# Packing diagonal score tiles and diagonal maxima tiles two to a set of four banks

## The chip, the core and the metric

The kernel runs on one core of one Trainium2 chip. The metric is the time of one execution in device microseconds (us); smaller is better. The engines are named as in the profile: PE is TensorE (PEld its weight loads), DVE is VectorE, ACT is ScalarE, POOL is GpSimd, and SP issues the DMAs. PSUM, into which PE writes, has eight banks of 512 float32 per partition here, called b0 to b7 in the kernel.

## The reference

One transformer block on 2048 tokens of 1024 features, in float32: layer norm with a modulation by a condition vector, causal attention with 32 query heads and 8 key heads of 32 features, a gated residual, a second modulated norm, and a low-rank mixture with one chosen expert of eight.

```python
mod = (_silu(L0_c) @ L0_wmod).reshape(L0_c.shape[0], 6, 1, -1)
...
h = _layernorm(x) * (1 + ca) + sa
q, k, v = h @ Wq, h @ Wk, h @ Wv          # 32 heads of q, 8 of k and v, head size 32
q, k = _apply_rope(q), _apply_rope(k)
scores = einsum('bhqd,bhkd->bhqk', q, k_h) / sqrt(32)
scores = where(causal, finfo.min, scores)  # key later than query is masked
ctx = einsum('bhqk,bhkd->bhqd', softmax(scores), v_h)
x = x + ga * (ctx @ Wo)
h = _layernorm(x) * (1 + cb) + sb
x = x + gb * low_rank_of_the_best_expert(h)
```

## The kernel before

The attention is done in 32 steps, one for each pair of a block of 512 queries (`qb`, 0 to 3) and a group of four heads (`m`, 0 to 7); `steps` holds them in the order of `qb`. In each product of the attention the four heads lie on four strips of 32 partitions, so that four matmuls of 32 partitions run beside each other, one for each head `j`, and each writes a bank of its own.

A step has these pieces, each known to the planner by a letter:

- **M, a visit of the maxima** (`unit` in `maxima_units`, L1406). It takes four banks, one for each head, computes the scores of one tile of 128 queries (`t`, 0 to 3) against 512 keys (`kc`), queries on partitions, and lets DVE reduce each bank to its row maxima (L1432). On the diagonal (`kc == qb`) only (t+1)·128 keys are computed: 128, 256, 384 or 512 columns. Before the products, 16 small bf16 matmuls write the mask of the diagonal 128x128 block (L1419); then L1426 adds the products.
- **R** (`shift_rows`): the maxima, negated and split into three bf16 parts by POOL (`split_maxima`, L1441 to L1447), are turned into rows by PE and copied by ACT (L1457).
- **S, a visit of the scores** (`weights`, L1472). It takes four banks and computes the scores again the other way round, 128 keys on partitions against 512 queries. L1479 writes minus the maximum with one matmul of bf16 ones for each head; on the diagonal L1487 adds the mask with 16 bf16 matmuls; L1492 adds the products. ACT takes the exponential of each bank into a tile `et` of SBUF (L1498). On the diagonal tile number `kc` begins at column `offset(kc)`: 0, 128, 256 or 384, so it is 512, 384, 256 or 128 columns wide. `nk` is the number of key tiles of a step: 4, 8, 12 or 16.
- **P** (`weighted_sum` and `accumulate`): PE multiplies `et` with the values into one bank `po` (L1508); POOL, in the last step DVE, adds `et` into `acc` (L1524 for the first two tiles, L1526 after that), except the last two tiles of a step.
- **D** (`denominators`, L1534): PE sums `acc` and the last two `et` tiles over the keys; then ACT, DVE and POOL divide (L1539, L1543, L1547).
- **F** and **T**: everything else of the block, cut into parts of some 0.4 to 1.9 us of PE: projections with the rotary turn (L675, L966, L844, L845), the output product (L675), transposes (L742), the second half of the block.

M and S use the array by rows: 32 partitions in, 128 columns out. P, D, R and most of F use it by columns: 128 partitions in, 32 columns out (the line's shape in the profile reads 32\*128 or 128\*32). The transposes use the whole array (128\*128). All float32 products go through the array in two passes, so that each appears twice in the profile's counts.

Buffers: `et` has four buffers (`epool`, bufs=4). A buffer comes free when POOL has added it and PE has used it; those of the last two tiles of a step come free with D. The eight banks are dealt out by the planner: an M or S takes four, P, D, R and F take one.

The order of the pieces is set before anything is issued by `plan_order` (L97), a beam search over states of the engines with a price for each piece, for each change of array form (`start`, L139), for each read of a bank and for each free buffer. It is the same order on all engines: PE, ACT, DVE and POOL each issue their instructions in it. `maxima` (L185), `scores` (L211), `sums` (L235) and `shares` (L258) are its pictures of M, S, P and D; `choices` (L327) tells which piece may come next, for instance S only while fewer than two scored tiles wait for their P (L340). The lists `ahead` and `tiles` (L1556 to L1566) tell it which M and S there are. The change alters the set of pieces, hence the search finds another order throughout.

Of the kernel before, what the change touches and what calls it, by code (L numbers as in the profile page):

```python
# [10 lines left out]
F32 = mybir.dt.float32  # L11
BF16 = mybir.dt.bfloat16
AF = mybir.ActivationFunctionType
# [83 lines left out]
def plan_order(parts, trail, steps, ahead, starts, tiles, ends, rates, gates):  # L97
# [87 lines left out]
    def maxima(s):  # L185
        n, t, kc = ahead[s[MAXIMA]]
        qb = steps[n][0]
        nk = QB if kc < qb else (t + 1) * P
        masked = kc == qb
        ready, turned = take(s, 4), unit_needs[s[MAXIMA]][1]  # L190
        if turned:
            ready = max(ready, s[TURNED][turned - 1] + TO_PE)
        s[PE] = start(s, "Rb" if masked else "R", ready) + 0.00167 * nk + (0.15 if masked else 0.0)
        s[WORK] += 0.00167 * nk
        after = s[PE] + TO_ENGINE
        give(s, *[(use(s, DVE, 0.07 + 0.00104 * nk, after) + TO_PE, b) for b in s[GOT]])
        s[MAXIMA] += 1
        if s[MAXIMA] - 1 == final[n]:
            done = use(s, POOL, 1.3, use(s, DVE, 0.15, 0.0) + BETWEEN)
            s[MINUS] = s[MINUS] + (done + TO_PE,)  # L200
# [10 lines left out]
    def scores(s):  # L211
        n, kc = tiles[s[SCORED]]
        if kc == 0:
            s[NOW] = n
            flush(s)
        width = QB - max(0, kc * P - steps[n][0] * QB)
        s[PE] = start(s, "Rb", max(take(s, 4), s[MINUS][n])) + 0.00209 * width
        s[WORK] += 0.00209 * width
        if kc >= 4 * steps[n][0]:
            s[PE] += 0.13  # L220
        free, s[ETS] = s[ETS][0], s[ETS][1:]
        after = max(s[PE] + TO_ENGINE, free)
        read = []
        for b in s[GOT]:
            done = use(s, ACT, 0.07 + 0.00083 * width, after)
            read.append((done + TO_PE, b))
        give(s, *read)
        s[READY] = s[READY][1:] + (done,)
        s[CREDIT] += rates[s[SCORED]]
        s[SCORED] += 1  # L230
# [4 lines left out]
    def sums(s):  # L235
        i = s[SUMMED]
        n, kc = tiles[i]
        nk = 4 * (steps[n][0] + 1)
        width = QB - max(0, kc * P - steps[n][0] * QB)
        ready = et_ready(s, i)  # L240
        at = ready + TO_PE
        if kc == 0:
            at = max(at, take(s, 1))
            s[SUM_BANK] = s[GOT][0]
        s[PE] = start(s, "C", at) + 0.00167 * width
        s[WORK] += 0.00167 * width
        if kc == nk - 1:
            give(s, (use(s, ACT, 0.5, s[PE] + TO_ENGINE) + TO_PE, s[SUM_BANK]))
        adder, us = (DVE, 0.0043) if n == last_step else (POOL, 0.00875)
        if kc == 1:  # L250
            s[ACC] = use(s, adder, us * QB, max(ready + BETWEEN, s[ACC_FREE]))
            free_et(s, max(s[ACC], s[PE]), 2)
        elif 1 < kc < nk - 2:
            s[ACC] = use(s, adder, us * width, ready + BETWEEN)
            free_et(s, max(s[ACC], s[PE]), 1)
        s[SUMMED] += 1
# [70 lines left out]
    def choices(s):  # L327
# [10 lines left out]
        if s[SCORED] < len(tiles):  # L338
            n, kc = tiles[s[SCORED]]
            if n < s[ROWS] and s[SCORED] - s[SUMMED] < 2 and not (s[SHARED] < n and kc > 1):  # L340
                found.append((max(four, s[MINUS][n] - 0.8), "S", scores))
        if s[SUMMED] < s[SCORED]:
            n, kc = tiles[s[SUMMED]]
            if not (s[SHARED] < n and kc == 1) and s[FILL] >= sums_need[s[SUMMED] > 0]:
                found.append((et_ready(s, s[SUMMED]) + TO_PE, "P", sums))
# [22 lines left out]
    for n, kc in tiles:  # L368
        span = starts[n + 2] - starts[n + 1] if n < last_step else 0.0
        due.append(starts[n + 1] + span * (kc + LEAD) / (4 * (steps[n][0] + 1)))  # L370
# [93 lines left out]
def adaln_block_kernel(  # L464
# [937 lines left out]
    def maxima_units(n):  # L1402

        qb, m = steps[n]

        def unit(t, kc):  # L1406
            nk = QB if kc < qb else (t + 1) * P
            if n not in maxima:
                maxima[n] = two.tile([P, 4, 4, NQB], F32, tag="mx", name=f"mx_{n}")
            mx = maxima[n]  # L1410
            q, k = quad(m, qb), k_t[:, m // 4, :]
            masked = kc == qb
            ps = score_banks(f"sm_{n}_{t}_{kc}")

            if masked:
                for s in range(4):
                    o = t * P + s * HD
                    for j, rows in groups:
                        nc.tensor.matmul(  # L1419
                            ps[j][:, o : o + HD], later[rows, s, :],  # L1420
                            pick[rows, s, s * HD : (s + 1) * HD], start=(s == 0), stop=False,
                        )
            spans = [(t * P, nk), (0, t * P)] if masked and t else [(0, nk)]
            for a, b in spans:
                for j, rows in groups:
                    nc.tensor.matmul(  # L1426
                        ps[j][:, a:b], q[rows, t * P : (t + 1) * P],
                        k[rows, kc * QB + a : kc * QB + b], start=not masked,
                        stop=(a, b) == spans[-1],
                    )  # L1430
            for j in range(4):
                nc.vector.tensor_reduce(mx[:, t, j : j + 1, kc], ps[j][:, :nk], AX.X, ALU.max)  # L1432

        units = [lambda t=t, kc=kc: unit(t, kc) for t in range(4) for kc in range(qb + 1)]
        return units

# [22 lines left out]
    class Attend:  # L1459
        def __init__(self, n):  # L1460
            self.n = n
            self.qb, self.m = steps[n]
            self.nk = 4 * (self.qb + 1)
            self.ets = {}

            last = n == len(steps) - 1
            self.adder = nc.vector if last else nc.gpsimd
# [4 lines left out]
        def weights(self, kc):  # L1472

            off, qb = self.offset(kc), self.qb
            q, k, nt = quad(self.m, qb), k_t[:, self.m // 4, :], nts[self.n % 2]
            ps = score_banks(f"sc_{self.n}_{kc}")

            for j, rows in groups:
                nc.tensor.matmul(  # L1479
                    ps[j][:, off:], ones_h[rows, :], nt[rows, off:],  # L1480
                    start=True, stop=False,
                )
            if kc >= 4 * qb:
                for s in range(4):
                    w = (s + 1) * HD
                    for j, rows in groups:
                        nc.tensor.matmul(  # L1487
                            ps[j][:, off : off + w],
                            pick[rows, s, :], later[rows, s, :w], start=False, stop=False,
                        )  # L1490
            for j, rows in groups:
                nc.tensor.matmul(  # L1492
                    ps[j][:, off:], k[rows, kc * P : (kc + 1) * P], q[rows, off:],
                    start=False, stop=True,
                )
            et = epool.tile([P, 4, QB], F32, tag="et", name=f"et_{self.n}_{kc}")
            for j in range(4):
                nc.scalar.activation(  # L1498
                    et[:, j, off:], ps[j][:, off:], AF.Exp, scale=1.0 / math.sqrt(HD)
                )  # L1500
            self.ets[kc] = et

        def weighted_sum(self, kc):
            off, et = self.offset(kc), self.ets[kc]
            if kc == 0:
                self.po = bank(f"po_{self.n}")
            for j, rows in groups:
# [3 lines left out]
                    start=(kc == 0), stop=(kc == self.nk - 1),  # L1511
                )
            if kc == self.nk - 1:
                nc.scalar.copy(quad(self.m, self.qb), self.po)

        def accumulate(self, kc):

            off, et = self.offset(kc), self.ets[kc]
            if kc == 1:
# [5 lines left out]
            elif 1 < kc < self.nk - 2:  # L1525
                self.adder.tensor_add(self.acc[:, :, off:], self.acc[:, :, off:], et[:, :, off:])  # L1526

        def denominators(self):
            pd = bank(f"pd_{self.n}")
            parts = [(0, self.acc)]  # L1530
            parts += [(self.offset(kc), self.ets[kc]) for kc in (self.nk - 2, self.nk - 1)]
# [25 lines left out]
    for n, (qb, m) in enumerate(steps):  # L1557
        ahead += [(n, t, kc) for t in range(4) for kc in range(qb + 1)]
# [7 lines left out]
    tiles = [(n, kc) for n in range(len(steps)) for kc in range(4 * (steps[n][0] + 1))]  # L1566
    attend = [Attend(n) for n in range(len(steps))]
    ends = [sum(s.nk for s in attend[: n + 1]) for n in range(len(steps))]
# [23 lines left out]
    for n, t, kc in ahead:  # L1592
        qb, m = steps[n]
        b = 2 * qb + t // 2
# [13 lines left out]
        parts, [k for k, _ in trail], steps, ahead, starts, tiles, ends, rates, gates  # L1608
# [5 lines left out]
    for letter, banks in order:  # L1614
# [15 lines left out]
        elif letter == "S":  # L1630
            n, kc = tiles[i]
            now[0] = n
            attend[n].weights(kc)
        elif letter == "P":
            n, kc = tiles[i]
# [68 lines left out]
```

## Time and profile before

| | |
|---|---|
| median of 3 runs | 1782.79 us (1782.09 to 1783.23) |
| the profiled execution | 1782.16 us |
| its span, first to last instruction | 1780.4 us |
| around the span | 1.8 us |
| PE busy | 1747.0 us (98%) |
| POOL busy | 1185.1 us (67%) |
| DVE busy | 1094.3 us (61%) |
| ACT busy | 740.0 us (42%) |
| mean granted clock of PE | 0.996 |

The span is what the profile covers; the time of an execution has 1.8 us more. Busy time is counted from the first to the last moment of an instruction, and the ends of matmuls are modelled, so a PE that is busy for 98% of the span may still spend part of that on filling and emptying the array. What a visit costs PE is better read from the timeline: from the start of its first matmul to the start of the first matmul after it.

### The profile page before, as it was taken

The page shows a single profiled execution, that of the slowest core. Times are in us where ns is not written, and L with a number is a line of the kernel's source. Part 1 is how long each engine was busy: PE and PEld are TensorE (multiplying, and loading weights), DVE is VectorE, ACT ScalarE, POOL GpSimd, SP SyncE. Part 2 cuts the span into 40 slices and gives each one's busy share as a digit, 9 for nine tenths or more (in the row PEclk, how much of TensorE's full clock was granted, in tenths as well). Part 3 has the DMA queues.
Part 4 walks back from the last instruction along what each step waited for, and adds up shares of the span by engine and source line. Part 5 has one row for each costly group of instructions (what it writes and reads, how often), then busy time and mean ns, then how long its engine had stood idle before and what let it go on. Part 6 is the DMA issues. An engine that isn't in the chain of part 4 may idle for free.

```text
span 1780.4 us, 55951 instructions
## 1 busy us (share of the span) xinstructions
PE 1747.0 (98%) x25112; PEld 708.9 (40%) x25112; DVE 1094.3 (61%) x2160; ACT 740.0 (42%) x1634; POOL 1185.1 (67%) x568
## 2 busy tenths in 40 slices
PE   7999999999999999999999999999999999999997
PEld 3655555444444333334444343333333333333333
DVE  2455456755755674676475566575566765666497
ACT  1203334344433424455444333454544444455452
POOL 1233343487567649657885866978979778798852
PEclk9999999999999999999999999999999999999999
DMA  9512323212422421131103011101102111110101
GB/s 350 181 30 74 115 80 103 73 50 62 137 73 96 153 87 49 49 102 61 61 26 125 26 49 68 41 37 49 49 25 73 37 61 49 49 49 25 49 13 49
DMA packets 68496, 130.57 MB, mean 73 GB/s; under 512 B 3744, under 2 KB 20768, under 8 KB 68256
## 3 DMA queue, kind: packets, MB, share of 16 engines
q1 hardware_dynamic: 66928, 125.85, 20.5%
q8 instruction: 196, 3.21, 0.8%
q10 hardware_dynamic: 1328, 1.15, 0.2%
q14 instruction: 44, 0.36, 0.1%
HBM read 118.59 MB, written 8.39 MB: 71 GB/s over the span
## 4 chain that ended last, share of the span: by engine, by line
PE 88%; POOL 6%; DVE 2%; issue 2%; DMA 1%; ACT 1%; POOLq 0%; ACTq 0%; DVEq 0%
PE sm L1426 15%; PE po L1508 14%; PE sc L1492 12%; PE pw L675 11%; PE pq L966 11%; PE sc L1479 5%; POOL acc L1526 5%; PE pd L1534 3%; PE pk L675 3%; PE pv L675 2%; PE pa L675 2%; PE open L966 2%; PE pf L675 2%; PE sm L1419 1%; DVE mx L1432 1%
## 5 line engine op out<-in xcount | busy, mean ns | idle before, releaser
L1432 DVE TENSOR_REDUCE mx<-sm 128x1 f32<-128x512 f32 (+3 forms) x1280 | 689.0, 602 | 397.7 <-PE sm L1426 396.2
L1498 ACT ACTIVATE et<-sc 128x512 f32<-128x512 f32 (+3 forms) x1280 | 578.4, 540 | 705.5 <-PE sc L1492 701.3
L1526 POOL TENSOR_TENSOR acc<-acc,et 128x2048 f32<-128x2048 f32 (+1 forms) x180 | 792.8, 4404 | 31.8 <-ACT et L1498 22.8
L1426 PE MATMUL sm<-k_t,q 32*128 32x512 f32 (+3 forms) x3328 | 336.6, 475 | 3.0 <-ACT et L1498 3.0
L1492 PE MATMUL sc<-q,k_t 32*128 32x512 f32 (+3 forms) x2560 | 297.2, 536 | 0.0
L1508 PE MATMUL po<-et,v_sb 128*32 128x512 f32 (+3 forms) x2560 | 294.8, 538 | 0.1
L675 PE MATMUL pw<-w,q 128*32 128x512 f32 x1920 | 238.7, 598 | 0.0
L1524 POOL TENSOR_TENSOR acc<-et,et 128x2048 f32<-128x2048 f32 (+1 forms) x31 | 132.1, 4261 | 98.5 <-ACT et L1498 83.1
L966 PE MATMUL pq<-h_t,w 128*32 128x256 f32 x3072 | 191.9, 384 | 0.0
L1426 PEld LDWEIGHTS sm<-k_t,q 32*128 32x128 f32 x3328 | 139.5, 184 | 116.9 <-issue 43.5
L966 PEld LDWEIGHTS pq<-h_t,w 128*32 128x32 f32 x3072 | 90.5, 110 | 100.6 <-issue 44.8
L1508 PEld LDWEIGHTS po<-et,v_sb 128*32 128x32 f32 x2560 | 59.0, 108 | 175.5 <-issue 152.3
L1543 DVE RECIPROCAL rd<-rd 128x128 f32<-128x128 f32 x128 | 112.4, 919 | 18.9 <-ACT rd L1539 18.8
L1479 PE MATMUL sc<-nt,ones_h 32*128 32x512 bf16 (+3 forms) x1280 | 120.1, 352 | 3.5 <-ACT rd L1539 2.9
L1112 POOL TENSOR_TENSOR x<-ag,x 128x512 f32<-128x512 f32 x40 | 60.9, 1523 | 87.3 <-DVE ag L1111 87.3
L1492 PEld LDWEIGHTS sc<-q,k_t 32*128 32x128 f32 x2560 | 115.5, 185 | 5.8 <-issue 2.1
L1479 PEld LDWEIGHTS <-ones_h 32*128 32x128 bf16 x1280 | 32.9, 91 | 207.6 <-issue 201.5
L844 POOL TENSOR_TENSOR swap_q<-swap_q,cs 128x512 f32<-128x512 f32 x32 | 40.9, 1277 | 105.7 <-DVE swap_q L841 105.7
L675 PEld LDWEIGHTS pw<-w,q 128*32 128x32 f32 x1920 | 50.1, 109 | 129.3 <-issue 110.8
L1547 POOL TENSOR_TENSOR q<-q,rd 128x512 f32<-128x512 f32 x31 | 41.6, 1343 | 67.3 <-DVE rd L1543 49.5
L1111 DVE TENSOR_TENSOR ag<-pw,gate 128x512 f32<-128x512 f32 x40 | 27.5, 687 | 62.5 <-PE pw L675 60.9
L844 POOL TENSOR_TENSOR swap_k<-swap_k,cs 128x512 f32<-128x512 f32 x8 | 10.2, 1276 | 82.7 <-DVE swap_k L841 82.7
(146 smaller groups left out, 1340.0 us busy)
## 6 DMA issues: line engine op xcount, KB each, us to landing
w<-in_wo_dram SPq DMA_DIRECT2D x112, 256.0 KB
w<-in_wmod_dram SPq DMA_DIRECT2D x48, 512.0 KB
w<-in_wq_dram SPq DMA_DIRECT2D x48, 512.0 KB
x<-in_x_dram SPq DMA_DIRECT2D x32, 512.0 KB
out_dram<-x SPq DMA_DIRECT2D x16, 512.0 KB
w<-in_wv_dram SPq DMA_DIRECT2D x12, 512.0 KB
w<-in_wk_dram SPq DMA_DIRECT2D x12, 512.0 KB
wq<-in_wq_dram SPq DMA_DIRECT2D x8, 512.0 KB
```

The costliest lines, as they stand in the source:

```text
L675: nc.tensor.matmul(dst[rows], left[:, rows], right, start=start, stop=stop)
L966: nc.tensor.matmul(ps[j * HD : (j + 1) * HD, a * TB : (a + 1) * TB], self.query_weights(half, k, j * P + h * HD), self.h_t[:, k, :], start ...
L1112: nc.gpsimd.tensor_add(x1[t][:, cols], tmp, x1[t][:, cols])
L1426: nc.tensor.matmul(ps[j][:, a:b], q[rows, t * P : (t + 1) * P], k[rows, kc * QB + a : kc * QB + b], start=not masked, stop=(a, b) == spans ...
L1432: nc.vector.tensor_reduce(mx[:, t, j : j + 1, kc], ps[j][:, :nk], AX.X, ALU.max)
L1479: nc.tensor.matmul(ps[j][:, off:], ones_h[rows, :], nt[rows, off:], start=True, stop=False,)
L1492: nc.tensor.matmul(ps[j][:, off:], k[rows, kc * P : (kc + 1) * P], q[rows, off:], start=False, stop=True,)
L1498: nc.scalar.activation(et[:, j, off:], ps[j][:, off:], AF.Exp, scale=1.0 / math.sqrt(HD))
L1508: nc.tensor.matmul(self.po[rows, off:], v_sb[:, kc, 4 * (self.m // 4) + j, :], et[:, j, off:], start=(kc == 0), stop=(kc == self.nk - 1),)
L1524: self.adder.tensor_add(self.acc[:, :, off:], first[:, :, off:], et[:, :, off:])
L1526: self.adder.tensor_add(self.acc[:, :, off:], self.acc[:, :, off:], et[:, :, off:])
L1543: nc.vector.reciprocal(part, part)
```

## The change

On the diagonal, pieces that do not fill their four banks are put together so that two of them fill one set of banks.

- Maxima: in all steps but the first two, query tile 0 (128 columns) and query tile 2 (384 columns) share one visit; tiles 1 and 3 stay alone. `unit` takes a tuple of tiles `ts`; `unit_list` names the visits. DVE still makes one reduction for each tile and head.
- Scores: in every step the key tiles nk-3 (384 columns) and nk-1 (128 columns) share one visit; the tile nk-2 (256 columns) comes after them. The narrow tile's columns lie at 384 to 511, the wide one's are moved to 0 to 383. Both `et` tiles are taken in this visit. ACT still makes one exponential for each tile and head. The P of the three tiles follow the new order.
- Planner: a visit may hold several tiles; it waits for all the `et` buffers that it needs, and S is offered only when that many are free. The mask's price in a maxima visit goes from 0.15 for each visit to 0.18 for each tile.

```diff
@@ plan_order: choices
-            n, kc = tiles[s[SCORED]]
-            if n < s[ROWS] and s[SCORED] - s[SUMMED] < 2 and not (s[SHARED] < n and kc > 1):
+            n, kc, _ = tiles[s[SCORED]]
+            k = packs[s[SCORED]]
+            if (
+                n < s[ROWS] and s[SCORED] - s[SUMMED] < 2 and not (s[SHARED] < n and kc + k > 2)
+                and len(s[ETS]) >= k
+            ):
                 found.append((max(four, s[MINUS][n] - 0.8), "S", scores))
@@ maxima_units: unit
-        def unit(t, kc):
-            nk = QB if kc < qb else (t + 1) * P
+        def unit(ts, kc):
...
-            ps = score_banks(f"sm_{n}_{t}_{kc}")
+            ps = score_banks(f"sm_{n}_{ts[0]}_{kc}")
+            runs, at = [], 0
+            for t in ts:
+                runs.append((t, at, at + ((t + 1) * P if masked else QB)))
+                at = runs[-1][2]
             if masked:
-                for s in range(4):
-                    o = t * P + s * HD
+                for t, at, _ in runs:
+                    for s in range(4):
+                        o = at + t * P + s * HD
...
             for j in range(4):
-                nc.vector.tensor_reduce(mx[:, t, j : j + 1, kc], ps[j][:, :nk], AX.X, ALU.max)
+                for t, a, b in runs:
+                    nc.vector.tensor_reduce(mx[:, t, j : j + 1, kc], ps[j][:, a:b], AX.X, ALU.max)
@@ unit_list (new)
+        qb = steps[n][0]
+        if n < 2:
+            return [((t,), 0) for t in range(4)]
+        out = []
+        for t in range(4):
+            out += [((t,), kc) for kc in range(qb)]
+            out += [((), ((1,), qb), ((0, 2), qb), ((3,), qb))[t]] if t else []
+        return out
@@ Attend
+            self.order = [*range(self.nk - 2), self.nk - 1, self.nk - 2]
+            self.packs = [[kc] for kc in self.order]
+            self.packs[-3:-1] = [self.order[-3:-1]]
...
-        def weights(self, kc):
+        def weights(self, kcs):
...
+            runs = [(kc, self.offset(kc), self.offset(kc), QB) for kc in kcs]
+            if len(runs) > 1:
+                kc, off, _, _ = runs[0]
+                runs[0] = (kc, off, 0, QB - off)
...
+            for kc in kcs:
+                self.ets[kc] = epool.tile([P, 4, QB], F32, tag="et", name=f"et_{n}_{kc}")
             for j in range(4):
-                nc.scalar.activation(
-                    et[:, j, off:], ps[j][:, off:], AF.Exp, scale=1.0 / math.sqrt(HD)
-                )
+                for kc, off, a, b in runs:
+                    nc.scalar.activation(
+                        self.ets[kc][:, j, off:], ps[j][:, a:b], AF.Exp, scale=1.0 / math.sqrt(HD)
+                    )
```

Within a shared visit the matmuls of one kind stand together: in S the bf16 ones of both tiles, then the masks of both, then the products of both; in M the masks of both, then the products of both.

## The prediction

> **What bounds the kernel now.** I read the page first: whose time is it?
>
> ```profile
> span 1780.4 us, 55951 instructions
> PE 1747.0 (98%) x25112; PEld 708.9 (40%) x25112; DVE 1094.3 (61%) x2160; ACT 740.0 (42%) x1634; POOL 1185.1 (67%) x568
> ...
> PE 88%; POOL 6%; DVE 2%; issue 2%; DMA 1%; ACT 1%; POOLq 0%; ACTq 0%; DVEq 0%
> ```
>
> PE is busy for 98% of the span and makes 88% of the chain that ended last; no other engine is near. The granted clock is 0.996 on the mean, so it cannot rise. PE's own time is therefore the time, and the question is what of it is not products. The change removes no matmul: the two programs, whose instruction order can be read without running them, both hold 15,636. It removes visits, so I read the timeline for what a visit costs beyond its columns. Each duration below is from a group's first start to the next group's first start.
>
> ```profile
> 818.13 0.40 PE L1479 MATMUL sc<-nt,ones_h 32*128 32x512 bf16 x4
> ...
> 819.52 1.50 PE L675 MATMUL pv<-w,h_t 128*32 128x256 f32 x24
> 820.95 1.14 PE L1426 MATMUL sm<-k_t,q 32*128 32x512 f32 x8
> ...
> 823.02 0.34 PE L1479 MATMUL sc<-nt,ones_h 32*128 32x384 bf16 x4
> ...
> 824.15 1.07 PE L1508 MATMUL po<-et,v_sb 128*32 128x512 f32 x8
> ...
> 826.90 2.37 PE L675 MATMUL pk<-h_t,w 128*32 128x256 f32 x40
> 829.20 0.29 PE L1479 MATMUL sc<-nt,ones_h 32*128 32x256 bf16 x4
> ```
>
> Leaving the column form: 24 records took 819.52 to 820.95, 1.43 us; 40 took 826.90 to 829.20, 2.30 us. So 8 records are 0.435 us, three times that is 1.305, and some 0.13 us is left each time before a row visit starts (0.139 in the trace's nanoseconds).
>
> ```profile
> 1309.66 0.40 PE L1479 MATMUL sc<-nt,ones_h 32*128 32x512 bf16 x4
> ...
> 1310.84 1.07 PE L675 MATMUL pw<-w,q 128*32 128x512 f32 x8
> ...
> 1313.35 0.40 PE L1479 MATMUL sc<-nt,ones_h 32*128 32x512 bf16 x4
> ...
> 1314.44 1.03 PE L1426 MATMUL sm<-k_t,q 32*128 32x512 f32 x8
> 1315.39 1.07 PE L1534 MATMUL pd<-acc,ones_p 128*32 128x512 f32 x8
> ```
>
> Leaving the row form: the same scores visit takes 1.18 us ahead of a column product, 1.09 us ahead of another row visit (1.183 and 1.084 in nanoseconds): 0.099 us. A full maxima visit took 0.955 us behind a row visit here and 1.071 us in the usual row behind column work: 0.115 us more, because it opens with float32 products. A scores visit, which opens with bf16, pays 0.009.
>
> Do two tiles side by side then really save this, with masks on both? One place shows it, two masked scores visits that follow each other:
>
> ```profile
> 236.70 0.40 PE L1479 MATMUL sc<-nt,ones_h 32*128 32x512 bf16 x4
> ...
> 238.00 0.33 PE L1479 MATMUL sc<-nt,ones_h 32*128 32x384 bf16 x4
> ...
> 239.11 1.27 PE L966 MATMUL pq<-h_t,w 128*32 128x256 f32 x17
> ```
>
> Together 2.41 us; apart 1.39 (818.13 to 819.52) and 1.13 (823.02 to 824.15), 2.52. The difference 0.11 is one way out and in again of the row form; masks and products add up.
>
> **The change part by part.**
>
> *Visits.* 30 steps lose one maxima visit each, 32 steps one scores visit each: 640 become 578. If each had stood alone between column runs, that were 62 x (0.139 + 0.099 + 0.009) = 15.3 us. But the search orders everything anew, so I count in the two orders. Runs of row work: 588 before, 536 after (52 fewer). Runs of column work: 588 and 543 (45 fewer). Whole-array transposes: 63 and 63. Maxima without a mask at the head of a row run: 165 and 170; scores at the head: 305 and 275. Sum: 52 x 0.099 = 5.1; 45 x 0.139 = 6.3; minus 5 x 0.115 = 0.6; plus 30 x 0.009 = 0.3. **11.1 us less on PE**, all on the path.
>
> Here a rule of the Trainium skill stands behind the row. "TensorEngine Tiling (Array Packing)", Key Properties, says that changing the tiling mode drains the array; "TensorE: Matmul & The Clock Gate", the phases on the wall clock, puts the drain at some 128 cycles, 53 ns at 2.4 GHz. An estimate by that page alone: 97 changes x 0.053 = 5.1 us. The rows show 139 and 99 ns, more than a drain; the trace's durations count.
>
> *Masks, products, weight loads*: the same instructions, costed at nothing more by the 2.41 us above. No row shows two maxima masks side by side; a maxima visit of 128 columns takes 0.516 us (0.302 beyond its 0.214 of columns), one of 384 columns 0.950 (0.308 beyond). From none to the 0.2 us of a mask lost again over 30 visits is 0 to +6 us; I take 0, by the scores' row.
>
> *DVE and ACT*: the same number of reductions and exponentials.
>
> ```profile
> L1432 DVE TENSOR_REDUCE mx<-sm 128x1 f32<-128x512 f32 x896 | 554.9, 682 | 279.3 <-PE sm L1426 278.3
> L1432 DVE TENSOR_REDUCE mx<-sm 128x1 f32<-128x384 f32 x128 | 62.3, 549 | 44.9 <-PE sm L1426 44.7
> L1432 DVE TENSOR_REDUCE mx<-sm 128x1 f32<-128x128 f32 x128 | 28.1, 281 | 32.9 <-PE sm L1426 32.7
> ```
>
> A shared maxima visit holds its last bank for 4 x (281 + 549) = 3.3 us of DVE, a full one for 4 x 682 = 2.7. The exponentials: 282 and 504 ns against 603, so 3.1 against 2.4 us. A rule speaks against the change here: "PSUM — Partial Sum Buffer", PSUM bank collisions, wants a bank guarded as a bank, not by address, so the narrow tile's readers start only when the wide tile is done as well. If every shared visit paid its 0.65 us on PE, 62 x 0.65 = 40 us. But the next row visit must stand close behind to feel it. Pairs of row visits with nothing between fall from 52 to 42, those with under 0.7 us of work between from 37 to 18, under 1.0 us from 214 to 209; some 60 of 577 are close, so 40 x 60 / 577 = 4 us at most. On the other side, 29 close pairs fewer, at 0.1 us each (the usual maxima behind scores takes 1.05 us against 0.955), give 3 us back. I take 0, with +4 and -3 for the range.
>
> *The added wait.* A shared scores visit needs two `et` buffers at once: its first exponentials need those freed by the sums nk-7 and nk-6. ACT runs in order: behind a waiting exponential stand the copies of L1457, L1514, L1539 and the other exponentials, and four banks stay taken, for which PE's next row visit waits. POOL's addition takes 4.5 us. In the timeline of before, in the 24 steps with `qb` over 0, addition nk-6 ended after the first exponential of tile nk-3 in 7 steps, by 0.4 to 3.8 us, 12 us in all. The new order puts 16.5 us of PE work between S of nk-6 and the shared visit, 13.8 before; with 2.7 us more room only 1.1 and 0.4 of the lags are left, under 2 us. Hidden by column work, mostly: I take 0, with +5 for the range. Without the cover it would be all 12.
>
> *The end of a step.* Its last exponentials are 256 wide now, not 128: 4 x (389 - 282) = 0.4 us later, ahead of P and D. Other work stands there on PE (in the last step 14 parts of the output product follow); without it, 32 x 0.4 = 14 us. I take 0.
>
> *Moved work.* Projections, weight loads on SP's queue and rotary work on POOL move with the order; DMA has 1% of the chain. What can change is where chance waits fall. Summed over all visits, PE took 43 us more than the usual durations of the same visits; 14 of that lie in the opening and the ending, 29 between, among them 5.2 us at 959 (ACT stood behind the rotary table's sign, L832, which came late) and 3.3 at 178 (ACT's L1539 behind POOL's L1547). These are dealt anew: 0, give or take 5.
>
> *Sum.* 1782.16 of the profiled execution (span 1780.4 and 1.8 around it) - 11.1 = 1771.1; that execution lay 0.6 below the median, so **1771.7**, which I round to 1771.5.
>
> **The rivals.**
> - *More than the count*: the big chance waits do not come back (-8) and close pairs give 3: 1761 to 1767. For it: fewer close pairs. Against: new orders bring new waits.
> - *The wait for `et` eats most of it*: +5 to +9, 1776 to 1781. For it: 7 late additions, POOL busy at 80% and more behind 1060 us. Against: the 2.7 us of room.
> - *Slower, by the same wait without room*: if POOL's addition nk-6 is late at every shared visit of the 24 by 1 us net of cover, +24 - 11 = +13, 1795. It decides from 11.1 / 24 = 0.46 us of net wait for each. Against: in 17 of 24 steps the addition was done in time, and work on PE lies between.
> - *It does not do what it says*: a second set of masks, or the stretch between bf16 and float32, costs a change of form again; then 1781 to 1784. Against: 2.41 us at 236.70.
>
> **How the numbers follow.** Count as worked: 0.60, 1767 to 1776. More: 0.19. Wait eats most: 0.11, of which 0.01 ends within 0.2%. No saving: 0.05. Slower: 0.05. A difference of 0.2%, 3.6 us, is about what a measurement of this kernel tells from none. Faster 0.60 + 0.19 + 0.10 = 0.89, same 0.05 + 0.01 = 0.06, slower 0.05. The range of 8 in 10 takes the likeliest case with the bounds above (+4, +5, -3, and 5 either way, not all at once): 1764 to 1779.
>
> **What would show it.** In the timeline after, a shared scores visit of 384 and 128 columns ahead of a column product should take 1.13 + 0.59 - 0.11 = 1.61 us (0.594 is the usual one of 128 columns), a shared maxima visit 0.95 + 0.52 - 0.10 to 0.11 = 1.36. Row runs: 536. PE's busy time falls by some 5 to 11 us. The groups L1432 and L1498 keep counts and means. Wrong: shared visits dearer by 0.1 or more (masks), ACT's idle time with POOL's L1526 as releaser (the `et` wait), or PE's row visits over their usual durations by clearly more than 29 us between opening and ending.

## The result, and the profile after

The changed kernel takes 1765.06 us (median of 5 runs, 1762.35 to 1766.24) against 1782.79 us before: a ratio of 0.9901, 95% interval 0.9888 to 0.9915, or 17.7 us less. The forecast was 1771.5, with a range of 1764 to 1779. The profiled execution took 1763.81 us, its span 1762.0, so span against span the change brought 18.4 us.

The page after, its span, the busy row and the chain by engine:

```profile
span 1762.0 us, 56024 instructions
PE 1728.6 (98%) x25112; PEld 718.8 (41%) x25112; DVE 1089.4 (62%) x2160; ACT 737.9 (42%) x1634; POOL 1176.2 (67%) x568
...
PE 78%; POOL 15%; issue 3%; DVE 1%; DMA 1%; ACT 1%; SPq 0%; POOLq 0%; ACTq 0%; DVEq 0%
```

PE's busy time fell by 18.4 us, as much as the span, with the same 25,112 records. PE stays the bound: the chain runs over POOL's additions for more of its length (15% for 6%), but PE is as full as before, 98%. The mean granted clock of this execution is 0.999, against 0.996 before.

The timeline of PE after, columns as before (start, length, engine, line, operation, operands, count), around one shared scores visit:

```profile
1004.01 0.40 PE L1521 MATMUL sc<-nt,ones_h 32*128 32x384 bf16 x8
1004.24 0.47 PE L1529 MATMUL sc<-later,pick 32*128 32x32 bf16 x32
1004.54 1.09 PE L1535 MATMUL sc<-q,k_t 32*128 32x384 f32 x16
1005.56 1.06 PE L1553 MATMUL po<-et,v_sb 128*32 128x512 f32 x8
```

Twice the ones, twice the masks, twice the products, and one way back into the column form: 1004.01 to 1005.56, 1.55 us (1.554 is the median of the 26 that stand between column runs). The prediction had worked out 1.61. A shared maxima visit:

```profile
985.18 0.37 PE L1434 MATMUL sm<-pick,later 32*128 32x32 bf16 x32
985.39 1.19 PE L1447 MATMUL sm<-k_t,q 32*128 32x128 f32 x24
986.51 1.72 PE L686 MATMUL pk<-h_t,w 128*32 128x256 f32 x28
```

985.18 to 986.51, 1.33 us (1.331 is the median of the 19 that stand so), where 1.36 was worked out. So both are cheaper than the sum of their parts, by 0.057 and 0.026 us.

The readers on DVE, groups of the reductions by shape (busy us, mean ns, idle before):

```profile
L1454 DVE TENSOR_REDUCE mx<-sm 128x1 f32<-128x512 f32 x896 | 554.5, 682 | 282.4 <-PE sm L1447 281.7
L1454 DVE TENSOR_REDUCE mx<-sm 128x1 f32<-128x384 f32 x128 | 69.4, 546 | 2.8 <-PE sm L1447 2.8
L1454 DVE TENSOR_REDUCE mx<-sm 128x1 f32<-128x128 f32 x128 | 35.5, 282 | 63.2 <-PE sm L1447 63.0
```

The counts are those of before and the means nearly so (682, 549 and 281 ns). DVE now waits 63 us ahead of the narrow reductions and 2.8 ahead of the wide ones (32.9 and 44.9 before), as it would if it started on both when the shared visit is done. Together the idle time ahead of the two did not grow: 77.8 us before, 66.0 now. On ACT the exponentials of the shared visits take a little longer than before: 515 ns for 504 at 384 columns, 309 for 282 at 128.

To tell work from waiting I took every visit or run of PE work in the traces (from its first start to the next one's first start) and fitted one duration for each record of a kind and width, one for each change of form and one for each kind of opening, over all traces of this study together, leaving out those off by more than 20 ns. The sum of these is called *usual*; what the trace took beyond it is called *waits*, opening and ending included. It is a fit, good to about 1 us between kernels, and stands in no view of the profile. The rest of the span, some 15 us, lies ahead of the first matmul and behind the start of the last run. (The prediction had 43 us of waits for the kernel before, by another count; only figures of one and the same count can be compared.)

| kernel | span us | usual us | waits us | median us |
|---|---|---|---|---|
| before | 1780.4 | 1707.7 | 57.5 | 1782.8 |
| after | 1762.0 | 1693.4 | 53.6 | 1765.1 |
| difference | -18.4 | -14.3 | -3.9 | -17.7 |

14.3 us are work that PE no longer does, 3.9 us are fewer waits. What this count calls waits includes time in which PE works at a lower granted clock, and that is where the 3.9 us seem to lie. The profile of before has two such stretches between the opening and the ending (95 to 1730 us), from 184.25 to 187.66 us and from 962.49 to 969.31, both at a granted clock of 0.50; the profile after has none there. Each follows, or begins within, a wait of some 3 us:

```profile
182.88 0.32 PE L1479 MATMUL sc<-nt,ones_h 32*128 32x384 bf16 x1 [2.94 <-ACT rd L1539]
...
183.98 2.58 PE L966 MATMUL pq<-h_t,w 128*32 128x256 f32 x24
...
963.48 2.24 PE L1426 MATMUL sm<-k_t,q 32*128 32x512 f32 x4 [3.00 <-ACT et L1498]
```

The 24 records at 183.98 take 2.58 us, while 24 records of the same shape take 1.50 at 819.52 in the prediction's lines. PE had work in 9.2 of these 10.2 us, so the lower clock cost some 4.6 us (an estimate: half of 9.2). Without it the waits are 52.9 us before and 53.6 after. The executions on record say the same: 33 of the kernel before, taken with experiments 1 to 4, have a mean clock of 0.995, and the time rises by some 1.3 us for each 0.001 of clock lost; the five of the changed kernel have 0.998. So some 4 of the 17.7 us go with the clock (an estimate: 0.003 at that rate). At the same clock, 0.997, three executions of before took 1779.55 to 1780.09 us and one of the changed kernel 1765.06, some 14.7 less.

### The profile page after: what moved, and what is told of

It reads as the page before. It is cut to its first block, busy times and chain, and to the rows that moved or that the text cites. A ratio compares the mean times of both kernels' runs of the same rounds, so it can differ in the third digit from the quotient of the medians.

```text
span 1762.0 us, 56024 instructions
## 1 busy us (share of the span) xinstructions
PE 1728.6 (98%) x25112; PEld 718.8 (41%) x25112; DVE 1089.4 (62%) x2160; ACT 737.9 (42%) x1634; POOL 1176.2 (67%) x568
## 4 chain that ended last, share of the span: by engine, by line
PE 78%; POOL 15%; issue 3%; DVE 1%; DMA 1%; ACT 1%; SPq 0%; POOLq 0%; ACTq 0%; DVEq 0%
PE sm L1447 13%; POOL acc L1571 12%; PE pq L977 12%; PE po L1553 11%; PE sc L1535 10%; PE pw L686 8%; PE sc L1521 4%; PE pv L686 3%; PE pd L1579 3%; PE pk L686 3%; PE open L977 2%; PE pa L686 2%; PE mr L792 1%; PE pf L686 1%; PE sm L1434 1%
## 5 line engine op out<-in xcount | busy, mean ns | idle before, releaser
L1447 PE MATMUL sm<-k_t,q 32*128 32x512 f32 (+3 forms) x3328 | 327.7, 473 | 0.0
L1535 PE MATMUL sc<-q,k_t 32*128 32x512 f32 (+3 forms) x2560 | 290.4, 533 | 0.5 <-issue 0.5
L686 PE MATMUL pw<-w,q 128*32 128x512 f32 x1920 | 234.7, 598 | 4.0 <-DMA w<-in_wo_dram 4.0
L977 PE MATMUL pq<-h_t,w 128*32 128x256 f32 x3072 | 186.8, 382 | 0.0
L1447 PEld LDWEIGHTS sm<-k_t,q 32*128 32x128 f32 x3328 | 135.6, 184 | 124.6 <-issue 50.9
L1123 POOL TENSOR_TENSOR x<-ag,x 128x512 f32<-128x512 f32 x40 | 53.0, 1325 | 134.2 <-DVE ag L1122 134.0
L1553 PEld LDWEIGHTS po<-et,v_sb 128*32 128x32 f32 x2560 | 63.9, 109 | 164.8 <-issue 140.3
L1521 PE MATMUL sc<-nt,ones_h 32*128 32x512 bf16 (+3 forms) x1280 | 114.0, 351 | 0.7 <-ACT rd L1584 0.4
L855 POOL TENSOR_TENSOR swap_k<-swap_k,cs 128x512 f32<-128x512 f32 x8 | 10.2, 1275 | 90.3 <-DVE swap_k L852 90.3
```

The costliest lines, as they stand in the source:

```text
L686: nc.tensor.matmul(dst[rows], left[:, rows], right, start=start, stop=stop)
L977: nc.tensor.matmul(ps[j * HD : (j + 1) * HD, a * TB : (a + 1) * TB], self.query_weights(half, k, j * P + h * HD), self.h_t[:, k, :], start ...
L1123: nc.gpsimd.tensor_add(x1[t][:, cols], tmp, x1[t][:, cols])
L1447: nc.tensor.matmul(ps[j][:, a:b], q[rows, t * P : (t + 1) * P], k[rows, kc * QB + o : kc * QB + o + b - a], start=not masked, stop=(t, a, ...
L1521: nc.tensor.matmul(ps[j][:, a:b], ones_h[rows, :], nt[rows, off:], start=(kc == kcs[0]), stop=False,)
L1535: nc.tensor.matmul(ps[j][:, a:b], k[rows, kc * P : (kc + 1) * P], q[rows, off:], start=False, stop=(kc == kcs[-1]),)
```

## The experiments

Three theories went in. **A**: PE does less changing of array form, some 11 us, and the shared visits are cheaper in themselves, some 2.5. **B**: the gain is the planner's, whose new price and new pieces made it find a better order. **C**: what is gained beyond the count comes from fewer row visits close behind each other, so less waiting for banks; against it **L**: that part is the luck of one order.

**1. The new price alone** (e1_price_only), on the kernel before:

```diff
-        s[PE] = start(s, "Rb" if masked else "R", ready) + 0.00167 * nk + (0.15 if masked else 0.0)
+        s[PE] = start(s, "Rb" if masked else "R", ready) + 0.00167 * nk + (0.18 if masked else 0.0)
```

> The kernel before with the planner's new mask price alone (0.18 for 0.15), no packing; the search finds another order. Theory A (the gain is the changes of array form that packing removes, some 11 us, and cheaper shared visits, some 2.5 us): its order has 595 row runs, 598 column runs and 65 transpose runs against 588, 588 and 63, so 2.4 us slower than before, 1785, give or take the 5 us by which chance waits are dealt anew. Theory B (the gain comes from the better price and the order found anew, packing only goes along): most of the 18 us, 1766 to 1772.

Measured: 1785.55 us, ratio 1.0017 (1.0011 to 1.0024); usual 1710.6, waits 60.4. That is where the count put it (1785). Theory B, in the form that the price alone did it, falls.

**2. Only the maxima packed** (e2_maxima_only), on the changed kernel:

```diff
-            self.order = [*range(self.nk - 2), self.nk - 1, self.nk - 2]
+            self.order = [*range(self.nk)]
             self.packs = [[kc] for kc in self.order]
-            self.packs[-3:-1] = [self.order[-3:-1]]
```

> The changed kernel with only the maxima packed; the scores are tile by tile in the old order of tiles. 570 row runs, 577 column runs, 64 transpose runs, 170 openings with an unmasked maxima visit. Theory A: 18 x 0.099 + 11 x 0.139 - 5 x 0.115 - 1 x 0.15 = 2.6 us by the count, and 30 shared maxima visits cheaper by 0.027 each, 0.8: 1779.4, give or take 5. Theory B: as fast as the changed kernel, near 1765. A third theory C (what packing frees is the banks: fewer close pairs of row visits, so less waiting): pairs with under 0.7 us between fall from 89 to 64, against 60 in the changed kernel, so nearly all of its 4 to 5 us of fewer waits, 1774 to 1776.

In the order found here R of step 4 stands ahead of the last S of step 2. Both steps keep their row of shifts in the same buffer (`nts[n % 2]`), so this S takes another step's shift and the output is wrong there; in experiment 7 it is so for R of steps 6 and 7. The planner has no rule against such an order. The number and sizes of the instructions are the same, so the two runs are used for their times alone. At the places concerned PE waits for such a row once, for 0.41 us (experiment 7, at 246 us).

Measured: 1781.29 us, 0.9992 (0.9984 to 1.0000). Usual 1703.9, 3.8 less than before, against 3.4 by the count; waits 62.3, 4.8 more. The work shrank as counted, and waits took most of it back; by the same estimate some 3 of the 4.8 us are the lower clock (17 us at 0.50 between opening and ending, 10.2 before). Theory C expected fewer waits for fewer close pairs (64 for 89); this speaks against it.

**3. Only the scores packed** (e3_scores_only):

```diff
-            out += [((), ((1,), qb), ((0, 2), qb), ((3,), qb))[t]] if t else []
+            out += [((t,), qb)]
```

> The changed kernel with only the scores packed; every diagonal maxima tile has its own visit. 557 row runs, 559 column runs, 66 transpose runs, 160 openings with an unmasked maxima visit. Theory A: 31 x 0.099 + 29 x 0.139 + 5 x 0.115 - 3 x 0.15 = 7.2 us by the count and 1.8 for 32 shared scores visits cheaper by 0.057: 1773.8, give or take 5. Theory B: near 1765. Theory C: close pairs (under 0.7 us) 77 against 89 before and 60 after: about half of the 4 to 5 us of fewer waits on top, 1771 to 1772.

Measured: 1774.24 us, 0.9954 (0.9942 to 0.9967); usual 1699.4 (8.3 less than before; the count said 9.0), waits 56.3. A holds. Together the two halves save 3.8 + 8.3 = 12.1 us of usual time, the whole 14.3.

**4. The change of form put back** (e4_form_change_put_back): same order, banks and reads as the changed kernel, and one small matmul in column form between the two masks.

```diff
             for kc, off, a, b in runs:
+                if kc != kcs[0]:
+                    nc.tensor.matmul(
+                        ps[0][:HD, :HD], zero_h, ident_h[:, :HD], start=False, stop=False
+                    )
                 for s in range(4) if kc >= 4 * qb else ():
```

and the same ahead of the second mask of a shared maxima visit.

> The changed kernel in its own order, with one small column-form matmul (a bf16 zero of 128 x 32 times 32 columns, added to a bank of the visit) between the two tiles' masks of each of the 62 shared visits. It puts one change of array form and back into each and leaves order, banks, reads and buffers alone. Theory A: 62 x (0.139 + 0.099 + some 0.02 for the matmul) = 14.8 to 16 us slower than the changed kernel, 1780 to 1781. Theory B or C (order or banks): 62 x 0.02 to 0.05 = 1 to 3 us, 1766 to 1768.

Measured: 1776.73 us, 0.9961 (0.9948 to 0.9975), some 11 us above the changed kernel. PE's timeline there, a scores visit:

```profile
1012.81 0.40 PE L1527 MATMUL sc<-nt,ones_h 32*128 32x384 bf16 x8
1013.04 0.32 PE L1539 MATMUL sc<-later,pick 32*128 32x32 bf16 x16
1013.29 0.19 PE L1533 MATMUL sc<-ident_h,zero_h 128*32 128x32 bf16 x1
1013.41 0.33 PE L1539 MATMUL sc<-later,pick 32*128 32x32 bf16 x16
1013.58 1.09 PE L1545 MATMUL sc<-q,k_t 32*128 32x384 f32 x16
1014.60 1.06 PE L1563 MATMUL po<-et,v_sb 128*32 128x512 f32 x8
```

A single matmul of 32 columns takes the visit from 1.554 to 1.79 us (1012.81 to 1014.60). Its own work is little of that: 32 masks of the row form, of 32 to 128 columns, took 0.30 us together in the visit at 1004.24. The shared scores visits grew by 0.231 us, the shared maxima visits by 0.163 (1.331 to 1.494), so 32 x 0.231 + 30 x 0.163 = 12.3 us. Order and banks were untouched, hence the cost is the form's own, as A says; but it was expected at 14.8 to 16 us. Between two stretches of bf16 masks a change and back, with the small matmul in it, costs 0.16 to 0.23, not the 0.238 that was read between float32 products. These are 62 changes and back; the change itself removed 52 ways out of the row form and 45 out of the column form, so the two sums are not one and the same.

**5. Tile by tile inside the visit** (e9_tile_by_tile_inside), on the changed kernel in its own order:

```diff
             for kc, off, a, b in runs:
                 for j, rows in groups:
                     nc.tensor.matmul(
                         ps[j][:, a:b], ones_h[rows, :], nt[rows, off:],
...
-            for kc, off, a, b in runs:
                 for s in range(4) if kc >= 4 * qb else ():
...
-            for kc, off, a, b in runs:
                 for j, rows in groups:
                     nc.tensor.matmul(
                         ps[j][:, a:b], k[rows, kc * P : (kc + 1) * P], q[rows, off:],
```

so that ones, masks and products of one tile come ahead of those of the other, and likewise in the maxima.

> The changed kernel in its own order, but inside each shared visit the matmuls stand tile by tile (ones, mask, products of the first tile, then of the second; in the maxima mask and products of the first, then of the second) instead of kind by kind. It asks where the shared visits' own cheapness comes from: 1.554 us for a shared scores visit where 1.611 was worked out, 1.331 for a shared maxima visit where 1.356 was. Theory G (it is the grouping by kind: fewer changes between bf16 and float32): shared visits go back to 1.61 and 1.36, 32 x 0.057 + 30 x 0.025 = 2.6 us slower than the changed kernel, 1767.5. Theory N (the grouping is nothing; the sum of the parts was misread): 1.554 and 1.331 as they are, 1765.

Measured: 1767.57 us, 0.9916 (0.9901 to 0.9931), 2.5 us above the changed kernel. A scores visit of it:

```profile
1007.93 0.34 PE L1524 MATMUL sc<-nt,ones_h 32*128 32x384 bf16 x4
...
1008.96 0.22 PE L1524 MATMUL sc<-nt,ones_h 32*128 32x128 bf16 x4
...
1009.56 1.07 PE L1554 MATMUL po<-et,v_sb 128*32 128x512 f32 x8
```

1007.93 to 1009.56, 1.63 us for 1.554; the shared maxima visit takes 1.358 for 1.331. Theory G holds by these rows: the grouping by kind makes the shared visits cheaper than their parts, 32 x 0.076 + 30 x 0.027 = 3.2 us. The times alone would not show it: the runs do not overlap (1767.21 to 1769.69 and 1762.35 to 1766.24), but the ratio intervals do by 0.0014, and the mean granted clock is 0.997 here for 0.998.

**6. Other orders of the same pieces.** The planner keeps the best 200 states at each stage. With another width it finds another order of the same work, before and after alike:

```diff
-    WIDTH, GRAIN = 200, 0.4
+    WIDTH, GRAIN = 100, 0.4
```

and the same with 400 and 1000, on both kernels.

> The changed kernel, its planner's beam 100 states wide instead of 200: the same pieces in another order. 533 row runs, 543 column runs, 63 transpose runs, 162 openings with an unmasked maxima visit. Count with the shared visits' own cheapness (2.6): 55 x 0.099 + 45 x 0.139 + 3 x 0.115 + 2.6 = 14.6 us below before, 1768.2, plus whatever its waits differ from those of before. Theory L (the changed kernel's 4.5 us of fewer waits are luck of one order): waits here are anything within 5 us of before's, 1763 to 1773, centre 1768. Theory C (fewer close pairs of row visits cause them; 64 here, 60 in the changed kernel, 89 before): again some 4 us fewer, 1763 to 1765.

> The changed kernel with a beam 400 wide. 538 row runs, 546 column runs, 64 transpose runs, 171 openings with an unmasked maxima visit: 50 x 0.099 + 42 x 0.139 - 6 x 0.115 - 0.15 + 2.6 = 12.6 us below before by count, 1770.2. Theory L: 1765 to 1775, centre 1770. Theory C (close pairs 55, the fewest): 4 to 5 us fewer waits, 1765 to 1766.

> The kernel before with a beam 100 wide: 591 row runs, 590 column runs, 65 transpose runs, 156 openings with an unmasked maxima visit: equal to before by count within 0.1 us. Theory L: 1778 to 1788 by its waits. Theory C (close pairs 91 against 89): the same waits, 1782 to 1784.

> The kernel before with a beam 400 wide: 591 row runs, 590 column runs, 66 transpose runs, 163 openings: 0.9 us above before by count. Theory L: 1779 to 1789 by its waits. Theory C (close pairs 90): 1783 to 1784.

> The changed kernel with a beam 1000 wide. 540 row runs, 547 column runs, 64 transpose runs, 167 openings with an unmasked maxima visit: 12.7 us below before by count (2.6 of it the shared visits' own cheapness), 1770, plus the difference in waits. If a wider beam finds orders with fewer waits (1766.8, 1765.1, 1760.4 at 100, 200, 400), 1757 to 1760; if the waits are chance, anything from 1759 to 1769.

> The kernel before with a beam 1000 wide. 592 row runs, 590 column runs, 68 transpose runs, 161 openings: 1.0 us above before by count. The packing's own worth is the difference to the changed kernel at the same beam: 20.7, 17.7 and 16.0 us so far at 100, 200 and 400; by count and cheapness alone 13.7 here. If the difference is 16 or more again, the changed kernel also waits less by nature; if 12 to 15, it does not. In time: 1773 to 1777 with the trend of the beam, 1779 to 1788 without.

| beam | before: us (ratio, interval) | usual, waits | changed: us (ratio, interval) | usual, waits | changed less before: us, usual, waits |
|---|---|---|---|---|---|
| 100 | 1787.46 (1.0025; 1.0017 to 1.0032) | 1709.3, 61.2 | 1766.76 (0.9909; 0.9895 to 0.9923) | 1693.4, 59.5 | -20.7, -15.9, -1.7 |
| 200 | 1782.79 | 1707.7, 57.5 | 1765.06 (0.9901; 0.9888 to 0.9915) | 1693.4, 53.6 | -17.7, -14.3, -3.9 |
| 400 | 1776.38 (0.9959; 0.9946 to 0.9971) | 1709.1, 51.3 | 1760.37 (0.9870; 0.9857 to 0.9884) | 1694.3, 50.2 | -16.0, -14.8, -1.1 |
| 1000 | 1763.33 (0.9889; 0.9873 to 0.9906) | 1709.7, 38.5 | 1758.14 (0.9861; 0.9846 to 0.9876) | 1695.0, 45.8 | -5.2, -14.7, +7.3 |

The ratios are to the kernel before at its own 200. Usual time falls by 14.3 to 15.9 us with the change at every width: that is the packing's own worth. The waits go from 61 to 38 us before and from 60 to 46 after: they belong to the order that the search came upon, and their difference has either sign (-3.9 at 200, +7.3 at 1000). The lower clock is a part of them, 0 to 6.7 us between opening and ending by the estimate above; without it their differences are -3.7, +0.7, -0.9 and +7.3 us. In time the packing is worth 5.2 to 20.7 us, according to the order. Theory C fails as a cause of fewer waits: the orders before at 100, 200 and 400 have 91, 89 and 90 close pairs, as counted in the orders, and 61, 58 and 51 us of waits. L holds. On the page of the kernel before at 1000, fewer waits show as a fuller PE:

```profile
span 1763.2 us, 55947 instructions
...
PE 1739.9 (99%) x25112; PEld 706.3 (40%) x25112; DVE 1096.3 (62%) x2160; ACT 740.3 (42%) x1634; POOL 1185.7 (67%) x568
```

It holds 11.3 us more of PE busy time than the changed kernel at 200 in nearly the same span (1763.2 and 1762.0). Expected for this kernel was 1773 to 1777 or more; that a wide search alone takes off some 20 us was missed.

Where the waits lie can be seen from PE's weight loads (who waited for whom: us in total, times, longest). A load can wait while PE still works, so these are not PE's lost time. Before:

```profile
PEld sm L1426 <- DVE mx L1432: 32.4, 50, 0.8
PEld sm L1426 <- ACT et L1498: 25.1, 36, 3.8
```

The same kernel at a beam of 1000:

```profile
PEld sm L1426 <- DVE mx L1432: 23.6, 36, 0.8
PEld sm L1426 <- ACT et L1498: 15.3, 29, 0.8
```

In both rows maxima visits wait for banks to be read; the wait of 3.8 us lies in the visit at 959 that the prediction named, and it is gone. That these rows make up the 19 us between the two kernels is not shown.

**7. Only the maxima packed, beam 400** (e12_maxima_only_beam_400):

> Only the maxima packed, with a beam 400 wide: 574 row runs, 576 column runs, 65 transpose runs, 173 openings with an unmasked maxima visit. Against the kernel before at the same beam (591, 590, 66, 163; 1776.4 us): 17 x 0.099 + 14 x 0.139 + 0.15 - 10 x 0.115 + 0.8 for the shared visits = 3.4 us less by the count, 1773.0, and anything within 5 us of it by chance waits. If the maxima's packing is worth nothing by nature (at a beam of 200 it brought 1.6 us), 1776 to 1777; if it is worth half of the whole, 1768.

Measured: 1763.54 us, 0.9895 (0.9878 to 0.9911), against 1776.4 before at 400. Usual 1704.4, 4.7 less than before at 400 (3.4 by the count); waits 42.5, 8.8 less. The expectation missed by 9.5 us; its own bound for chance waits, 5 us, was too small. With experiment 2 it shows the same pieces worth 1.6 or 12.8 us in time (11.4 by the two ratios, since the runs at 400 were not taken together) and 3.8 or 4.7 in usual time.

The fastest version is the changed kernel at a beam of 1000: 1758.14 us, a ratio of 0.9861.

## Why the prediction was right, and where its size was off

*Fewer changes of form, 11.1 us.* Right in mechanism: one change and back put into each of the 62 shared visits (experiment 4) cost 12.3 us by the rows, some 11 in time. The split counts of experiments 1, 2 and 3 came within 1 us of the usual time of the fit, and at all four widths the packing takes 14.3 to 15.9 us of usual time, of which the count and the next item make 13.7.

*The rule on drains.* "TensorEngine Tiling (Array Packing)", Key Properties, says that changing the tiling mode drains the array, and experiment 4 agrees that a change of form costs. The estimate by the drain of "TensorE: Matmul & The Clock Gate", phases on the wall clock, 53 ns, gave 5.1 us in all. Experiment 4 has 0.231 and 0.163 us for a change and back, 116 and 82 ns each, above 53. The measurement decides.

*A clock that cannot rise.* This reading was wrong. The mean granted clock went from 0.996 to 0.999 in the profiles and from 0.995 to 0.998 on the mean of the executions. That was worth some 4 us by the estimate under the result, and the sum has no term for it.

*Masks and products add up, 0.* This is the first term that was mis-sized: the shared visits are 32 x 0.057 + 30 x 0.026 = 2.6 us cheaper than their parts. The row that it rested on, two masked visits in a row at 236.70, alternates bf16 and float32 tile by tile; the changed code groups by kind, and experiment 5 shows that this is the difference. The bound for the maxima's masks was 0 to +6, on the wrong side of nothing.

*Longer held banks, 0, with +4 and -3.* Right within its bounds: shared visits did not make waits grow, and three of the four widths have fewer after. The rule that a bank is guarded whole ("PSUM — Partial Sum Buffer", PSUM bank collisions) fits DVE's rows, with 63 us of idle time ahead of the narrow reductions; no cost of it to PE can be told in the table of widths. The fewer waits expected from fewer close pairs (-3) were not borne out.

*The wait for `et`, 0.* On ACT it came to more than the 2 us worked out. Who waited for POOL's additions after the change:

```profile
  ACT et L1543: 6.7, 6
```

Six waits, 6.7 us; before, ACT had no such wait in its rows by shape. At the end of a step the weight loads of D waited for the same additions for 6.4 us (1.8 before). It did not decide: the rival of a slower kernel needed 0.46 us of net wait at each of 24 shared visits, 11 us on PE, and PE's waits as a whole are 53.6 us for 57.5.

*Chance waits, 0 give or take 5.* It came to -3.9, within that bound, and this part is luck of the order. The two long waits of before are gone, and with them the stretches at half clock, which the prediction had taken for waiting; a new wait of 4.7 us came at 667, at a run of output products whose weights were late. It has three parts (1.04, 1.50 and 1.51 us), of which this is the first, and no stretch at half clock followed:

```profile
672.91 1.07 PE L686 MATMUL pw<-w,q 128*32 128x512 f32 x8 [1.04 <-DMA w<-in_wo_dram]
```

The spread was given too small: four widths of the beam give the kernel before 38 to 61 us of waits, 23 us from end to end. At 400 and 1000 the changed kernel lies below the forecast range, at 1760.37 and 1758.14 us.

*Sum.* 11.1 as predicted, 2.6 for the grouping and 3.9 for the waits make 17.6 of the 18.4 us of span; 0.8 is left to the fit and to what lies outside the visits. The likeliest case was therefore right in its cause, and the case called "more than the count" (1761 to 1767) is the one that came true, for half the reason that it named: the big waits did go, fewer close pairs did not count, and the grouping by kind was not foreseen.

## What to carry to other kernels

Count the changes of array form in the two instruction orders and price each from the timeline (first start to next first start); that gave the work to within some 3 us where the busy share (98%) says nothing. When two tiles share a visit, group the matmuls by kind: here that alone was worth some 3 us of the 17.7. And where a search sets the order, compare versions at several settings of the search: one order's waits differ from the next by as much as the edit is worth, and a wider search alone took some 20 us off the kernel before. Look at the granted clock of each execution as well: 0.003 of it went with some 4 us here, as much as the waits did.

## What was not expected of the hardware

A bf16 matmul of 32 columns in the other array form lengthens a scores visit by 0.23 us and a maxima visit by 0.16 us. The first is as much as all the bf16 ones of a shared scores visit, 512 columns for each head (1013.04 less 1012.81 in experiment 4's lines, 0.23 us). And the order of bf16 and float32 products within one form has a price: 0.076 us for going from float32 back to bf16 once in a shared scores visit, 0.027 us in a shared maxima visit (1.630 for 1.554, 1.358 for 1.331).

A long wait of PE was paid twice. In the fourteen traces PE stood idle for 2.9 us or more at a time seven times between opening and ending (2.9 to 4.6 us, two of them in the kernel before), and each time a stretch of 3.4 or 6.8 us at a granted clock of 0.50 began within 5 us of the start of the wait. Shorter or broken waits had it in some cases (experiment 4, at 680.6 us) and not in others (after, at 672 to 678).
